# Moving small work between engines and timing every step by a table, in a two-layer graph kernel on one core

## The chip, the core and the metric

The kernel runs on one core of a Trainium2 chip. The core has a matmul engine (PE, with its weight loads as PEld), a vector engine (DVE), a scalar engine for activation functions (ACT), a general engine (POOL) and a queue for transfers (SP). Each works through its own instructions in program order and waits on semaphores for the others. The metric is the device time of one execution in microseconds; lower is better. Times come from three runs of the kernel, and one further execution was profiled.

## The reference

The input x has 32 batches of 512 channels by 1024 nodes; adj is a 512 by 512 matrix. Two layers follow each other, both on a layer norm over the nodes with a relu, and both with a residual:

```python
# layer 0
h = jnp.maximum(_layernorm(x, axis=-1), 0.0)
q = jnp.einsum('c,bcn->bn', wq, h)
k = jnp.einsum('c,bcn->bn', wk, h)
scores = q[:, None, :] + k[:, :, None]
scores = jnp.where(scores > 0, scores, 0.01 * scores)
att = jax.nn.softmax(scores, axis=-1)
agg = jnp.einsum('bcn,bmn->bcm', h, att)
out = jnp.einsum('oc,bcm->bom', adj, agg) + bm[None, :, None]
x = x + jax.nn.relu(out)
# layer 1
h = jnp.maximum(_layernorm(x, axis=-1), 0.0)
W = adj * adj
x = x + jnp.einsum('bnf,nm->bmf', h, W) + bias
```

## The kernel before, in words

A score is a leaky relu of q[n] + k[m]. For one row m the nodes n split into those with q[n] above -k[m] and those below, and in each part the exponential is a product of a factor of n and a factor of m. So the kernel sorts the nodes by q and needs, for each row, a sum over the nodes above a rank and another over those below. No 1024 by 1024 matrix of scores is made.

One batch goes through these steps, each a small function:

- load (four blocks of 128 channels), stats, norm, slopes, relu: layer norm and relu of layer 0, in place.
- scores and columns: q and k by matmuls, copied to the tile qr (line 216), through memory to all partitions (qrow), and transposed to columns (qk).
- rank (eight times): the place of each node in the order, by comparisons of qrow with a column of qk. Line 260 settles ties; it reads two tensors in on-chip memory, a slice of qrow and the mask before. lower (eight times, ACT, line 267): how many q lie below -k, by sums of signs.
- factors, to_rows, from_rows: small arithmetic that turns ranks into rows of a table td in memory (index idx) and into the rows to be read later (idg).
- value (eight times, PE, line 314): adj times h, 128 nodes at a time; spread copies it out of PSUM to the tile v; scatter (POOL, line 327) writes its rows, with q in the last column, to td in sorted order.
- fetch (SP, line 344): the sorted rows come back in nine groups, held in three tiles vs. weights: the factors of the nodes, as exponentials of the last column, copied first to the tile q (lines 351, 352). later: with w the weights, e is the sum of w over all later groups, made of eight additions one after another (line 369); wc are the weights with a one for the carry.
- totals: the running denominators by matmuls with masks, copied to den. stationary (POOL, line 387, three times): masks times weights, the stationary operand sm of three scans.
- scan (nine times, PE, line 397): a running sum of one group from above and of one from below, 64 partitions each. sums (nine times): ACT copies the two carries into the next groups' rows (lines 407, 408), then the whole result to the tile t (line 410); DVE copies the denominator into its last column (line 411); SP writes t to td (lines 413, 414).
- gather (POOL, eight times, line 419): for each node its row of running sums. excess and divide: the coefficients cf, with one exponential on ACT (line 430). combine (eight times): one multiplication on ACT (line 444), then two multiply-adds on DVE (line 446).
- turn (PE, line 453): transposes back; DVE adds the result, cut at zero, to the x that reload has brought again (tile y).
- stats, norm, slopes, relu for layer 1 (tile h); lift (POOL, line 205): adds bias to y; propagate (eight times, PE, line 460): W times h; finish (DVE, line 468): adds it to y, and SP writes y out.

Five batches are in the pipeline at once. The order of all instructions is written by hand: every step of batch b is put on a list with a planned time b * T + t, the list is sorted, and the steps are issued in this order, each engine's share of it being that engine's program. The planned times order the work and do nothing else. T is 80.57. In the last batches the late steps are moved forward by LAST and LAST_GAIN.

Buffers that matter here: PSUM has 8 banks, which all PE results share; t has 2 buffers, x and y have 7 tiles each of one channel block, g (the gathered rows of one batch) has one.

## Time and profile before

| What | us |
|---|---|
| median of three runs | 2488.57 (2484.91 to 2489.2) |
| the profiled execution | 2487.21 |
| its span, first to last instruction | 2485.5 |
| PE busy, granted clock 0.979 | 2358.2 |
| DVE busy | 2162.8 |
| ACT busy | 1458.2 |
| POOL busy | 992.7 |

The profile of one execution gives, for each engine, when each instruction ran. A group is a set of instructions of one line: after the bar come its busy time, the mean ns of one, then the idle time of the engine just before them and what ended most of it. A matmul in full precision appears as two passes, so value and propagate of one step are 8 records each. The records of a scan lie over each other; a scan takes 1.01 us from start to start. In 40 equal slices of the span, the busy tenths of three engines and the granted clock are:

```profile
PE   5789999999999999999999999999999999999788
DVE  6578999999999999999999999999999898888754
ACT  3666556566656566556566656566656566656441
...
PEclk9889999999999999999999999999999999999988
```

The transfers move 642.92 MB, at 259 GB/s in the mean, and the 16 transfer engines are busy for eight to nine tenths of most slices.

### The profile page before, as it was taken

How to read it: one execution, taken by the hardware profiler on the slowest of the kernel's cores; microseconds unless marked ns; L12 is line 12 of the kernel's file. 1: busy time of each engine (PE TensorE's matmuls, PEld its weight loads, DVE VectorE, ACT ScalarE, POOL GpSimd, SP SyncE). 2: the span in 40 equal slices, each digit the busy share in tenths (PEclk: the TensorE clock that was granted, in tenths of full speed). 3: DMA queues.
4: the chain of work that ended last, by engine and by line, in shares of the span. 5: the costliest groups of instructions: out<-in, count | busy, mean ns of one | idle time of the engine just before them, and what ended most of it. 6: DMA issues, size and time to landing. Idle time of an engine off the chain costs nothing. (4 is left out here: it accounts for less than half of the span.)

```text
span 2485.5 us, 28977 instructions
## 1 busy us (share of the span) xinstructions
PE 2358.2 (95%) x7632; PEld 991.0 (40%) x7632; DVE 2162.8 (87%) x5649; ACT 1458.2 (59%) x2341; POOL 992.7 (40%) x1101
## 2 busy tenths in 40 slices
PE   5789999999999999999999999999999999999788
PEld 2233444443444443344443444444344443444333
DVE  6578999999999999999999999999999898888754
ACT  3666556566656566556566656566656566656441
POOL 1234433344434334434334433345443334543431
PEclk9889999999999999999999999999999999999988
DMA  4698889898889888889888889898888888888772
GB/s 148 170 290 271 270 270 269 262 277 285 267 277 285 238 273 276 264 267 284 258 269 269 273 266 286 241 279 274 272 270 279 255 269 265 262 279 268 224 258 85
DMA packets 206528, 642.92 MB, mean 259 GB/s; under 512 B 29030, under 2 KB 29158, under 8 KB 206364
## 3 DMA queue, kind: packets, MB, share of 16 engines
q1 hardware_dynamic: 146704, 370.65, 53.9%
q0 software_dynamic: 57344, 268.99, 28.7%
q10 hardware_dynamic: 2316, 1.43, 0.3%
q8 instruction: 62, 1.02, 0.2%
q14 instruction: 102, 0.84, 0.1%
HBM read 429.94 MB, written 211.02 MB: 258 GB/s over the span
## 5 line engine op out<-in xcount | busy, mean ns | idle before, releaser
L460 PE MATMUL pg<-h,wsq 128*128 128x512 f32 x2048 | 936.8, 606 | 18.9 <-ACT h L199 18.6
L314 PE MATMUL pv<-wmT,x 128*128 128x512 f32 x2048 | 927.2, 601 | 24.3 <-ACT x L199 24.3
L419 POOL DMA_INDIRECT g<-td,idg x256 | 245.6, 959 | 1055.9 <-DVE e L369 498.0
L460 PEld LDWEIGHTS pg<-h,wsq 128*128 128x128 f32 x2048 | 378.8, 192 | 553.7 <-issue 462.8
L314 PEld LDWEIGHTS pv<-wmT,x 128*128 128x128 f32 x2048 | 375.2, 191 | 494.0 <-issue 444.8
L397 PE MATMUL sc<-vs,sm 128*64 128x512 f32 x1152 | 344.3, 636 | 67.6 <-ACT vs L407 49.2
L327 POOL DMA_INDIRECT td<-v,idx x256 | 275.8, 1077 | 319.8 <-issue 225.0
L446 DVE SCALAR_TENSOR_TENSOR g<-g,cf 128x512 f32<-128x512 f32 x512 | 375.4, 746 | 16.6 <-ACT g L444 7.6
L260 DVE SCALAR_TENSOR_TENSOR junk<-qrow,qk,before 128x128 bf16<-128x128 f32 x256 | 337.6, 1319 | 9.1
L205 POOL TENSOR_TENSOR y<-y,bias_sb 128x1024 f32<-128x1024 f32 x128 | 300.4, 2359 | 33.8 <-issue 30.6
L321 ACT COPY v<-pv 128x512 f32<-128x512 f32 x256 | 148.1, 579 | 275.8 <-PE pv L314 200.5
L267 ACT ACTIVATE junk<-qrow,qk 128x1024 bf16<-128x1024 f32 x256 | 292.5, 1142 | 0.1
L199 ACT ACTIVATE x<-x,nmr,rstd 128x1024 f32<-128x1024 f32 x128 | 151.7, 1236 | 138.2 <-DVE nmr L192 138.2
L468 DVE SCALAR_TENSOR_TENSOR y<-pg,bm_sb,y 128x512 f32<-128x512 f32 x256 | 188.2, 744 | 25.7 <-PE pg L460 25.7
L410 ACT COPY t<-sc 128x512 f32<-128x512 f32 x288 | 168.5, 585 | 45.8 <-PE sc L397 13.8
L256 DVE TENSOR_SCALAR_CACHE_REDUCE junk<-qrow,qk,cnt 128x896 bf16<-128x896 f32 (+6 forms) x224 | 180.5, 806 | 8.2
L455 DVE SCALAR_TENSOR_TENSOR y<-tr,nbm,y 128x512 f32<-128x512 f32 x256 | 177.8, 726 | 7.9 <-PE tr L453 7.9
L397 PEld LDWEIGHTS sc<-vs,sm 128*64 128x64 f32 x1152 | 66.1, 137 | 290.2 <-issue 122.5
L407 ACT COPY vs<-sc 1x512 f32<-1x512 f32 x256 | 144.6, 565 | 62.9 <-PE sc L397 62.9
L444 ACT ACTIVATE g<-g,cf 128x512 f32<-128x512 f32 x256 | 173.2, 715 | 3.2 <-DVE cf L438 3.2
L251 DVE TENSOR_SCALAR_CACHE_REDUCE junk<-qrow,qk 128x128 bf16<-128x128 f32 (+6 forms) x224 | 166.9, 745 | 3.5
L181 DVE BATCH_NORM_STATS2 st<-x 128x6 f32<-128x512 f32 x256 | 162.2, 675 | 3.5 <-DMA x<-in_x_dram 3.4
(106 smaller groups left out, 1885.2 us busy)
## 6 DMA issues: line engine op xcount, KB each, us to landing
vs<-td SPq DMA_DIRECT2D x192, 384.8 KB
td<-t SPq DMA_DIRECT2D x576, 128.2 KB
x<-in_x_dram SPq DMA_DIRECT2D x128, 512.0 KB
y<-in_x_dram SPq DMA_DIRECT2D x128, 512.0 KB
out_dram<-y SPq DMA_DIRECT2D x128, 512.0 KB
qrow<-qd SPq DMA_DIRECT2D x32, 512.0 KB
td<-v,idx POOLq DMA_INDIRECT x256, 5.3
g<-td,idg POOLq DMA_INDIRECT x256, 8.7
```

The costliest lines, as they stand in the source:

```text
L205: nc.gpsimd.tensor_tensor(s.x[c], s.x[c], bias_sb, ALU.add)
L256: nc.vector.tensor_scalar(junk[:, j * P :], s.qrow[:, j * P :], qc, first, ALU.is_lt, ALU.add, accum_out=s.cnt[:, 1, j : j + 1],)
L260: nc.vector.scalar_tensor_tensor(junk[:, ts(j, P)], s.qrow[:, ts(j, P)], qc, before, ALU.is_equal, ALU.mult, accum_out=s.cnt[:, 2, j : j + 1],
L267: nc.scalar.activation(junk, s.qrow, AF.Sign, bias=s.qk[:, 1, j : j + 1], accum_out=s.sgn[:, j : j + 1])
L314: nc.tensor.matmul(pv, s.h[c][:, ts(j, P)], wmT[:, c, :], start=(c == 0), stop=(c == NC - 1))
L327: i = nc.gpsimd.indirect_dma_start(tds[s.b % 3][:, :], bass.IndirectOffsetOnAxis(ap=s.idx[j // 4][:, j % 4 : j % 4 + 1], axis=0), v[:, :], ...
L397: nc.tensor.matmul(p[ts(k, HP), :], s.sm[i][k], s.vs[h][:, 0:C], start=True, stop=True)
L419: nc.gpsimd.indirect_dma_start(s.g[:, j, :], None, tds[s.b % 3][0 : 3 * NB * HP, :].rearrange("(s k) w -> s (k w)", k=3), bass.IndirectOff ...
L446: nc.vector.scalar_tensor_tensor(r, s.g[:, j, k * W : k * W + C], s.cf[:, k, j : j + 1], r, ALU.mult, ALU.add)
L455: nc.vector.scalar_tensor_tensor(xh, pt, nbm[:, o : o + 1], xh, ALU.max, ALU.add)
L460: nc.tensor.matmul(pg, wsq[:, r, ts(c, P)], s.h[r][:, ts(i, HALF)], start=(r == 0), stop=(r == NC - 1),)
L468: nc.vector.scalar_tensor_tensor(xh, s.pg.pop((c, i)), bm_sb[:, c : c + 1], xh, ALU.add, ALU.add)
```

## The change

Six edits. The bias addition lift goes from POOL to DVE. The copy of raw scores to qr goes from DVE to ACT. weights takes its exponentials straight from the fetched rows, six on ACT with three columns each instead of six copies and two exponentials; the weights are now kept in the opposite order of groups, with a zero in front of each half. later makes its sums over groups with one scan instruction. The denominator's copy into t goes from DVE to ACT. combine is split into weigh (ACT) and two separate multiply-adds (DVE). And every single step has a planned time of its own in a table, with T = 79.96, shifts for the first five batches and new ones for the last three; one load of batch 1 uses a buffer of y.

```diff
+PLAN = {
...
+    "excess": (197.53,),
...
+    "fetch": (74.37,),
...
+    "gather": (166.9, 167.4, 174.29, 175.46, 169.28, 190.2, 170.94, 177.02),
...
+    "norm0": (-13.33,),
+    "norm1": (246.23,),
...
+    "scan": (90.8, 98.9, 110.43, 116.3, 124.4, 137.24, 146.6, 154.57, 156.26),
...
+    "stationary": (87.74, 100.59, 124.44),
...
+    "sums": (91.04, 103.93, 115.73, 121.32, 128.67, 145.61, 149.72, 155.13, 157.36),
...
+    "turn": (230.81, 230.13, 230.45, 232.2, 233.84, 234.71, 233.3, 233.76),
...
+}
+LAST = (0.94, 0.36, 0.02,)
+LAST_KNOTS = (60, 95, 130, 150, 215, 250, 275, 300, 345, 400)
+LAST_GAIN = (0, 1.2, 5.7, 20.4, 20.4, 46.5, 53, 74.2, 87.6, 87.6)
+FIRST_KNOTS = (-60, 60, 150, 250, 350)
+FIRST_SHIFT = (
+    (1.7, -1.4, -0.5, -1.8, -0.5),
...
+)
...
+    zero = const.tile([P, 2], F32, name="zero")
+    nc.vector.memset(zero, 0.0)
+    runs = const.tile([P, 2 * (NB + 1)], F32, name="runs")
+    nc.vector.memset(runs, 1.0)
+    nc.vector.memset(runs[:, NB + 1 : NB + 2], 0.0)
...
     def load(s, c):
-        t = xp.tile([P, N], F32, tag="x", name=f"x_{s.b}_{c}")
+        pool, tag = (yp, "y") if (s.b, c) == (1, NC - 1) else (xp, "x")
+        t = pool.tile([P, N], F32, tag=tag, name=f"x_{s.b}_{c}")
...
     def lift(s, c):
-        nc.gpsimd.tensor_tensor(s.x[c], s.x[c], bias_sb, ALU.add)
+        nc.vector.tensor_tensor(s.x[c], s.x[c], bias_sb, ALU.add)
...
-        nc.vector.tensor_copy(s.qr, pq)
+        nc.scalar.copy(s.qr, pq)
...
     def weights(s):
-        q = sp.tile([P, 2, NB], F32, tag="q", name=f"q_{s.b}")
+        s.wz = sp.tile([P, 2, NB + 1], F32, tag="w", name=f"w_{s.b}")
+        s.w = s.wz[:, :, 1:]
+        nc.scalar.copy(s.wz[:, :, 0], zero)
         for i, t in enumerate(s.vt):
-            nc.vector.tensor_copy(q[:, 0, ts(i, 3)], t[:, :, C])
-            nc.vector.tensor_copy(q[:, 1, ts(NB // 3 - 1 - i, 3)], t[:, ::-1, C])
-        s.w = sp.tile([P, 2, NB], F32, tag="w", name=f"w_{s.b}")
-        nc.scalar.activation(s.w[:, 0, :], q[:, 0, :], AF.Exp, bias=s.nq[:, 0:1])
-        nc.scalar.activation(
-            s.w[:, 1, :], q[:, 1, :], AF.Exp, bias=s.nq[:, 1:2], scale=SLOPE
-        )
+            nc.scalar.activation(
+                s.w[:, 0, ts(NB // 3 - 1 - i, 3)], t[:, ::-1, C], AF.Exp, bias=s.nq[:, 0:1]
+            )
+            nc.scalar.activation(
+                s.w[:, 1, ts(i, 3)], t[:, :, C], AF.Exp, bias=s.nq[:, 1:2], scale=SLOPE
+            )
...
-        s.e = e = sp.tile([P, 2, NB], F32, tag="e", name=f"e_{s.b}")
-        nc.vector.memset(e, 0.0)
-        for h in range(NB - 2, -1, -1):
-            nc.vector.tensor_tensor(
-                e[:, :, h : h + 1], e[:, :, h + 1 : h + 2], s.w[:, :, h + 1 : h + 2], ALU.add
-            )
+        s.e = sp.tile([P, 2, NB + 1], F32, tag="e", name=f"e_{s.b}")
+        nc.vector.tensor_tensor_scan(
+            s.e.rearrange("p k g -> p (k g)"), runs, s.wz.rearrange("p k g -> p (k g)"),
+            0.0, ALU.mult, ALU.add,
+        )
...
-        nc.vector.tensor_copy(t[:, C:W], s.den[:, ha : ha + 1])
+        nc.scalar.copy(t[:, C:W], s.den[:, i : i + 1])
...
-    def combine(s, j):
+    def weigh(s, j):
         r = s.g[:, j, 0:C]
         nc.scalar.mul(r, r, s.cf[:, 0, j : j + 1])
-        for k in (1, 2):
-            nc.vector.scalar_tensor_tensor(
-                r, s.g[:, j, k * W : k * W + C], s.cf[:, k, j : j + 1], r, ALU.mult, ALU.add
-            )
+
+    def combine(s, j, k):
+        r = s.g[:, j, 0:C]
+        nc.vector.scalar_tensor_tensor(
+            r, s.g[:, j, k * W : k * W + C], s.cf[:, k, j : j + 1], r, ALU.mult, ALU.add
+        )
...
-    T = 80.57
+    def plan(s, f, name, *lead, args=None):
+        for n, t in enumerate(PLAN[name]):
+            at(s, t, f, s, *lead, *(args[n] if args else (n,)))
...
+    T = 79.96
```

In the order that the new table gives for a batch in the middle, PE runs, from its scores on: scores, value 3, columns, value 0, value 2, totals and scan 0 of the batch before, value 1, value 6, scan 1, value 7, value 4, value 5, then propagates and scans 2 to 6 in turn, a last pair of propagates among the transposes, scan 7, the transposes of one tile, scan 8. POOL runs gather 0, gather 1, stationary 0, then more gathers, stationary 3, the last gather and the scatters. In the order before, PE has its scans at even distances of 7.63 planned us, and POOL runs gather 0, then stationary 0, then the other gathers with three lifts among them.

## Prediction

> **What bounds the kernel now.** I read the page first: the busy shares and the costliest groups, then three stretches (start, middle, end), then the order of time in one period of the middle, then the waits of the middle. The page:

> ```profile
> span 2485.5 us, 28977 instructions
> PE 2358.2 (95%) x7632; PEld 991.0 (40%) x7632; DVE 2162.8 (87%) x5649; ACT 1458.2 (59%) x2341; POOL 992.7 (40%) x1101
> ...
> L260 DVE SCALAR_TENSOR_TENSOR junk<-qrow,qk,before 128x128 bf16<-128x128 f32 x256 | 337.6, 1319 | 9.1
> L205 POOL TENSOR_TENSOR y<-y,bias_sb 128x1024 f32<-128x1024 f32 x128 | 300.4, 2359 | 33.8 <-issue 30.6
> ```

> PE is full and DVE nearly so. One DVE group stands out: L260 reads only 128 columns and yet has a mean of 1319 ns; the list of its line gives a median of 354 and a maximum of 5374. The stretches (busy us of PE, PEld, DVE, ACT, POOL, then clock, DMA share, GB/s):

> ```profile
> 0.00:265.00 265.00, 211.72 (x680) 88.24 (x684) 190.59 (x585) 149.86 (x238) 78.59 (x115) 0.91 0.74 220
> 265.00:2266.00 2001.00, 1965.80 (x6425) 824.90 (x6423) 1838.64 (x4751) 1223.03 (x1971) 836.80 (x918) 0.99 0.87 270
> 2266.00:2486.00 220.00, 180.69 (x532) 77.83 (x530) 133.58 (x316) 85.28 (x132) 77.34 (x68) 0.91 0.61 206
> ```

> The middle holds 27 periods (first score matmul of batch 4 at 264.9, of batch 31 at 2266.5), 74.1 us each, with PE 98% busy. The order of time in one of them shows what PE still loses:

> ```profile
> 1247.87 5.36 DVE L260 SCALAR_TENSOR_TENSOR junk<-qrow,qk,before 128x128 bf16<-128x128 f32 x1
> ...
> 1264.97 2.36 POOL L205 TENSOR_TENSOR y<-y,bias_sb 128x1024 f32<-128x1024 f32 x1
> ...
> 1265.96 1.98 DVE L260 SCALAR_TENSOR_TENSOR junk<-qrow,qk,before 128x128 bf16<-128x128 f32 x1
> ...
> 1267.87 0.46 DVE L428 TENSOR_TENSOR cf<-g,arg 128x8 f32<-128x8 f32 x1
> ...
> 1268.56 0.21 ACT L430 ACTIVATE cf<-cf 128x8 f32<-128x8 f32 x1 [3.46 <-DVE cf L429]
> ...
> 1269.81 0.56 ACT L407 COPY vs<-sc 1x512 f32<-1x512 f32 x1
> ...
> 1270.42 1.67 PE L397 MATMUL sc<-vs,sm 128*64 128x512 f32 x4 [1.65 <-ACT vs L407]
> ```

> Read it downwards. A lift on POOL holds L260 on DVE (the 5.36 us one lies beside two lifts that run from 1248.39 to 1253.07). DVE comes late to the step excess (L428), ACT stands 3.46 us in its exponential (L430), the carry copies (L407) behind it come late, and scan 4 on PE waits 1.65 us. The waits of 300 to 2200 us say that it is so in every batch:

> ```profile
> PE sc L397 <- ACT vs L407: 32.1, 25, 3.5
> ACT cf L430 <- DVE cf L429: 92.0, 26, 5.1
> ```

> [...]

> **The parts of the change, per batch.**

> Lift moved from POOL to DVE. POOL loses 4 x 2.36 = 9.4 us. L260 falls from 1319 to about 354 ns: 8 x 0.965 = 7.7 us off DVE. DVE gains 4 x 1.22 = 4.9 us. If the price is wrong, 2.4 us (POOL's own) is the upper end: DVE then is up 1.9 net instead of down 2.8.

> Block sums as one scan. It removes 8 adds of 221 ns (L369) and a memset of 73: 1.8 us of busy time, 2.6 us of a dependent chain in the order of time. The scan instruction is in no row: between 0.15 (a one-column copy, L411) and 1.8 us (no gain); I take 0.3, for 20 columns.

> Raw scores and exponentials on ACT. DVE loses six copies of L351/L352 (0.93) and nine of L411 (1.3), and the score copy L216 (0.38). ACT gains the score copy, nine one-column copies, a zero copy and four more exponentials. The nearest row for the small ones is 0.19 to 0.30 (the accumulator read of L267 to L354), but back to back they stand about 0.1 to 0.2 apart: 0.3 + 9 x 0.12 + 0.1 + 4 x 0.2 = 2.3 us. In the new table the two square roots (norm0 66.6, norm1 6.4, in the period) no longer lie together between exponentials: weights 4.8, norm1, factors 34.9, norm0. That is four table loads instead of two, 2.6 us.

> Sums. DVE: 67.6 (2162.8/32) - 7.7 + 4.9 - 1.8 + 0.3 - 2.6 = 60.7 us. ACT: 45.6 + 4.9 = 50.5. POOL: 31.0 - 9.4 = 21.6. PE's instructions are the same, so PE is the bound, and only its stalls and order count.

> The table of all steps. I sorted both tables by time. PE's stream, without waits: 64 passes of value and of propagate at 0.43 us each, 9 scans of 1.01, 32 transposes of 0.109, scores 1.86, columns and totals 0.6, about 0.19 for each value or propagate that follows a scan or scores (9 before, 8 now): 71.6 us before, 71.4 now. So 2.5 us of 74.1 are loss today: 1.7 at scan 4 (shown above), 0.4 of clock (20 us at half clock in the middle, over 27), 0.4 of the rest.

> What is late next? I laid the new order out by hand, with the spacings of the order of time, PE from the start of scores at 0. DVE, 7 us lighter, has excess done at 37.5 and ACT asks for it at 39.2, so the stall at scan 4 should go. PE wants scan 0 at 13.0, scan 2 at 36, scan 5 at 49.6, scan 6 at 54.2, scan 7 at 68.8. ACT from scan 0 on is nearly unbroken (with relus at 1.14, sign sums at 1.14, sums at 1.8, spread at 0.48, weigh at 0.63): it reaches sums 4 at 47.2 and sums 5 at 52.6, so scan 6 has its carries at 53.8, 0.4 before PE wants them. Scan 8 has only the last transpose group (0.44) between itself and scan 7. In the trace a scan of 1.08, 0.07 to ACT, 0.61 to the first matmul of the next and 1.67 for that one give 3.4 us against 2.6 unhindered: a new stall of 0.85 us in each batch. With 0.4 of clock and 0.5 for the rest: 71.4 + 0.85 + 0.9 = 73.2 us, 0.9 less than now; 27 x 0.9 = 24 us.

> Start and end. The last batch's own chain loses 2.3 us in later, about 1 in weights (the copies) and some 2 of the lifts beside its ranks: 5 us. The new start shifts (FIRST_SHIFT) and the load of batch 1 into the y pool I cost at nothing, between -10 and +10: the first stretch has 53 us without PE, 28 of them before its first matmul and 24 lost to half clock, which no order removes. SP's queue: the load of block 3 of the next batch now stands in front of the rows of sums 2 and waits for value 5, the last reader of its buffer, at 32.5; sums 2 comes at 37, so it costs nothing. The fetch moves from 33 planned us ahead of scan 0 to 16; by my layout it is issued from 58 to 62, the one at 1289 to 1293 in the trace takes some 13 us to land, and weights wants it at 75, with 6 us more before scan 0 would wait: nothing, up to 1 us per batch if it lands at 82. PSUM: at most 7 of 8 banks are held at once in the new order (3 before), so no wait is forced there.

> Together 24 + 5 = 29 us: 2487.2 (the profiled execution; span 2485.5) - 29 = 2458. The median of the runs is 1.4 us higher: 2460.

> **Rivals.**

> Slower: POOL's queue. In the new order gather 0 and gather 1 of the older batch stand in front of stationary 0, whose product scan 0 needs. Gather 0 waits until the rows of sums 8 have landed: 7.7 us in the median from their last issue to gather 0, over the 32 batches (in the period above SP at 1227.24, POOL at 1234.60), the longest 9.9. By my layout the issue is 1.35 us after the end of scan 8, so gather 0 starts at 9.0, two gathers take 2.2, stationary 1.0: 12.3, and PE is there at 13.0. The slack is 0.7 us. From a landing of 8.4 us on, all of PE stands. At 10 us it costs 1.6 us per batch more: 74.8 instead of 73.2, 27 x 0.7 = 19 over now, less 5: 2502. For it: DMA is 0.87 busy, and the new order sends 1 MB of y tiles and the fetch shortly before. Against: 27 of the 32 are under 8.4.

> The same: ACT's chain. If sums 5 is 1.3 us later than laid out, scan 6 waits 0.9 us and the gain of the middle is gone: 2488 - 5 = 2484. Two things can do it: the nine small copies at 0.2 instead of 0.12 (0.5 by then), and t, which has two buffers: the copies of sums 4 need the landing of sums 2, which by the 7.7 us comes at 48, about when ACT asks. Against: the carries are copied before t.

> Much faster: the stall at scan 8 is covered, because ACT works ahead and PE never catches up elsewhere, and the residue halves: 72.1 us, 27 x 2 = 54, and 5 to 10 at the ends: 2427. For it: every engine but PE has over 12 us of room.

> **How the numbers follow.** Forecast 0.47 (2440 to 2478), much faster 0.20, ACT's chain 0.10 (2474 to 2492), POOL's queue 0.23. A measurement of this kernel tells 0.2% (5 us) from no change. The ACT rival is split 0.03 faster, 0.05 same, 0.02 slower; of POOL's queue 0.01 ends in same. Faster 0.70, same 0.06, slower 0.24. The predicted time is 2460; the range goes from the much faster case, 2425, to the worst landing, 2502.

> **What would show it.** In the new profile: the L260 group near 360 ns; lift on DVE at 1.2 to 1.3 us; DVE near 60.7 us x 32 = 1940 busy; ACT near 1620; table loads near 128 (67 and two singles before); the wait of the scan matmuls for L407 moved to one scan per batch, the last; PE busy share up by about 1%. The forecast is wrong if scan matmuls wait for POOL (then it is the queue), if DVE stays above 2050, or if the period is above 74.

## The result and the profile after

| | Before | After |
|---|---|---|
| median of the runs, us | 2488.49 (4 runs) | 2415.81 (4 runs) |
| span of the profiled execution, us | 2485.5 | 2415.1 |
| PE, DVE, ACT, POOL busy, us | 2358, 2163, 1458, 993 | 2344, 1932, 1591, 705 |
| granted clock, mean | 0.979 | 0.984 |

The ratio is 0.9708 (95% interval 0.9691 to 0.9724): 73 us less, where 28 were forecast, and below the range. The page of the changed kernel, the lines that answer to those of before:

```profile
span 2415.1 us, 28224 instructions
PE 2343.5 (97%) x7632; PEld 986.1 (41%) x7632; DVE 1932.3 (80%) x5012; ACT 1591.2 (66%) x2879; POOL 704.7 (29%) x973
...
L263 DVE TENSOR_TENSOR y<-y,bias_sb 128x1024 f32<-128x1024 f32 x128 | 153.4, 1220 | 4.5 <-ACT h L257 4.5
```

Its groups, with shapes kept apart (count, then busy us and mean ns):

```profile
L318 DVE SCALAR_TENSOR_TENSOR junk<-qrow,qk,before 128x128 bf16<-128x128 f32 x256 | 94.4, 369 | 9.1
L426 DVE TENSOR_TENSOR_SCAN e<-runs,w 128x20 f32<-128x20 f32 x32 | 6.1, 191 | 0.0
```

The tie step (L260 before, L318 now) takes 369 ns instead of 1319, the lift 1220 ns on DVE, the scan instruction 191 ns. The three stretches, cut at the first score matmul of batch 4 and of batch 31 (columns as before):

```profile
0.00:259.00 259.00, 210.43 (x668) 85.67 (x668) 172.84 (x512) 156.10 (x284) 70.94 (x111) 0.89 0.74 225
259.00:2209.00 1950.00, 1948.09 (x6430) 820.78 (x6429) 1619.74 (x4211) 1343.14 (x2431) 592.16 (x810) 1.00 0.88 277
2209.00:2416.00 207.00, 184.95 (x540) 79.67 (x538) 139.69 (x292) 91.96 (x165) 41.61 (x52) 0.95 0.63 217
```

The middle of 27 periods fell from 2001.6 to 1949.7 us, 51.9 less; PE is busy for 1948 of 1950 us, at a granted clock of 1.00. From batch 8 on the periods are 72.3 us each, but for the last, 71.6. In the old order one value (3.5 us) precedes the scores of its batch and in the new one none; with that set right, the start gained 264.9 - 3.5 - 259.3 = 2.1 us and the end 219.0 + 3.5 - 206.1 = 16.4. The sum is the 70.4 by which the span fell.

The waits of 300 to 2200 us (total, times, longest):

```profile
POOL sm L445 <- PE sc L455: 135.8, 26, 5.8
...
ACT cf L488 <- DVE cf L487: 4.4, 2, 2.2
```

ACT's wait for excess, 92 us before, is 4.4. POOL waits for scans of PE to give up a buffer of sm; no scan waits for POOL. What PE still loses shows in the order of time at the end of a period:

```profile
1266.14 1.08 PE L455 MATMUL sc<-vs,sm 128*64 128x512 f32 x4
1267.15 0.66 PE L513 MATMUL tr<-ident,g 128*128 128x128 f32 x4
1267.27 0.58 ACT L465 COPY vs<-sc 1x512 f32<-1x512 f32 x1 [8.14 <-PE sc L455]
...
1267.87 0.58 ACT L466 COPY vs<-sc 1x512 f32<-1x512 f32 x1
...
1267.90 1.67 PE L455 MATMUL sc<-vs,sm 128*64 128x512 f32 x4
...
1268.50 0.19 PEld L455 LDWEIGHTS sc<-vs,sm 128*64 128x64 f32 x2 [0.41 <-ACT vs L466]
```

Scan 7, one group of transposes, then scan 8, which starts when the first carry is copied and takes 1.67 us instead of 1.08 because its second half waits for the second one (L466). PE stands idle for less than 0.1 us before it, so nearly all of this stall of 0.7 us lies in the length of the scan and counts as busy. The prediction laid it out at 0.85.

### The profile page after: what moved, and what is told of

Read it like the earlier page. It is cut to its first block, busy times and chain, and to the rows that moved or that the text cites. A ratio compares the mean times of both kernels' runs of the same rounds, so it can differ in the third digit from the quotient of the medians.

```text
span 2415.1 us, 28224 instructions
## 1 busy us (share of the span) xinstructions
PE 2343.5 (97%) x7632; PEld 986.1 (41%) x7632; DVE 1932.3 (80%) x5012; ACT 1591.2 (66%) x2879; POOL 704.7 (29%) x973
## 4 chain that ended last, share of the span: by engine, by line
PE 92%; ACT 2%; DMA 2%; DVE 1%; issue 1%; POOL 0%; SPq 0%; ACTq 0%; POOLq 0%; DVEq 0%
PE pv L372 37%; PE pg L520 35%; PE sc L455 13%; PE tr L513 4%; PE pq L269 2%; DMA vs<-td 1%; ACT vs L465 1%; DMA g<-td,idg 1%; ACT x L257 1%; ACT g L502 0%; DVE y L515 0%; DMA td<-pad 0%; PE pd L434 0%; PE pr L283 0%; DMA bm_sb<-in_L_gnn_bm_dram 0%
## 5 line engine op out<-in xcount | busy, mean ns | idle before, releaser
L372 PE MATMUL pv<-wmT,x 128*128 128x512 f32 x2048 | 912.0, 599 | 0.0
L385 POOL DMA_INDIRECT td<-v,idx x256 | 286.7, 1120 | 571.2 <-ACT g L502 186.5
L465 ACT COPY vs<-sc 1x512 f32<-1x512 f32 x256 | 145.7, 569 | 418.1 <-PE sc L455 417.8
L506 DVE SCALAR_TENSOR_TENSOR g<-g,cf 128x512 f32<-128x512 f32 x512 | 350.0, 747 | 24.8 <-ACT g L502 24.5
L314 DVE TENSOR_SCALAR_CACHE_REDUCE junk<-qrow,qk,cnt 128x640 bf16<-128x640 f32 (+6 forms) x224 | 180.5, 806 | 8.2
L309 DVE TENSOR_SCALAR_CACHE_REDUCE junk<-qrow,qk 128x384 bf16<-128x384 f32 (+6 forms) x224 | 165.9, 740 | 9.3 <-DMA qrow<-qd 7.9
L502 ACT ACTIVATE g<-g,cf 128x512 f32<-128x512 f32 x256 | 163.9, 715 | 2.6 <-DVE cf L496 2.6
L239 DVE BATCH_NORM_STATS2 st<-y 128x6 f32<-128x512 f32 x256 | 160.6, 669 | 0.0
L263 DVE TENSOR_TENSOR y<-y,bias_sb 128x1024 f32<-128x1024 f32 x128 | 153.4, 1220 | 4.5 <-ACT h L257 4.5
L466 ACT COPY vs<-sc 1x512 f32<-1x512 f32 x256 | 147.7, 577 | 5.5
L257 ACT ACTIVATE h<-y,nmr,rstd 128x1024 f32<-128x1024 f32 x128 | 149.2, 1237 | 2.9 <-PE pg L520 2.3
```

Of the source, the lines that this page charges most:

```text
L239: nc.vector.bn_stats(st[:, i, :], s.x[c][:, ts(i, HALF)])
L257: nc.scalar.activation(h, s.x[c], AF.Relu, bias=s.nmr[:, c : c + 1], scale=s.rstd[:, c : c + 1])
L314: nc.vector.tensor_scalar(junk[:, j * P :], s.qrow[:, j * P :], qc, first, ALU.is_lt, ALU.add, accum_out=s.cnt[:, 1, j : j + 1],)
L372: nc.tensor.matmul(pv, s.h[c][:, ts(j, P)], wmT[:, c, :], start=(c == 0), stop=(c == NC - 1))
L385: i = nc.gpsimd.indirect_dma_start(tds[s.b % 3][:, :], bass.IndirectOffsetOnAxis(ap=s.idx[j // 4][:, j % 4 : j % 4 + 1], axis=0), v[:, :], ...
L506: nc.vector.scalar_tensor_tensor(r, s.g[:, j, k * W : k * W + C], s.cf[:, k, j : j + 1], r, ALU.mult, ALU.add)
```

## The experiments

Two theories stood at the start. By the first (placement), the lifts on POOL, which hold the tie step on DVE, are the cause of the loss before, and taking them off POOL is the gain. By the second (order), the table is the gain. The prediction and two of the expectations call the scan that waits in the kernel before scan 4; counted from 0 as everywhere else it is scan 5. The matmuls of totals, which stand behind scan 0 in the old order, follow the first scan of the period (1239.31 us), and the one that waits at 1270.42 is the sixth.

Each ratio is to the kernel before as it ran beside the changed one, with medians of 2482.9 to 2487.9 us. A few us between two rows lie inside the intervals; where they matter, the periods of the traces decide.

| Kernel | Median, us | Ratio to before (95%) | Middle period, us |
|---|---|---|---|
| e1 lift only, old order | 2421.0 | 0.9741 (0.9704 to 0.9779) | 71.8 |
| e2 changed, lift back on POOL | 2419.7 | 0.9736 (0.9698 to 0.9774) | 72.3 |
| e3 table only | 2438.0 | 0.9812 (0.9774 to 0.9851) | 72.3 |
| e4 all placements, old order | 2419.0 | 0.9731 (0.9693 to 0.9770) | 71.8 |
| e5 changed, scan 7 earlier | 2400.2 | 0.9662 (0.9644 to 0.9681) | 71.6 |
| e6 other placements, old order | 2480.0 | 0.9981 (0.9966 to 0.9996) | 73 to 76 |
| e9 changed, no end shifts | 2444.3 | 0.9834 (0.9793 to 0.9875) | 72.3 |
| e10 changed, no start shifts | 2420.3 | 0.9741 (0.9700 to 0.9782) | 72.3 |
| e11 changed, additions back | 2416.7 | 0.9728 (0.9688 to 0.9769) | 72.3 |
| e12 as e4, no end shifts | 2432.5 | 0.9778 (0.9758 to 0.9797) | 71.8 |

**e1: lift alone.**

```diff
-        nc.gpsimd.tensor_tensor(s.x[c], s.x[c], bias_sb, ALU.add)
+        nc.vector.tensor_tensor(s.x[c], s.x[c], bias_sb, ALU.add)
```

> The kernel before with only lift moved to DVE, the old order kept. Placement theory (lifts on POOL held the tie step L260 on DVE, and through excess and the carries scan 4): L260 falls to about 0.36 us in the mean, the stall of 1.7 us at scan 4 goes, the middle period falls from 74.1 to about 72.5 us, 2440 to 2455 us in all. Order theory (the table brings the gain, the placement only makes room): period within 0.4 us of 74.1, 2478 to 2490.

Measured 2421.0, a larger gain than the placement theory asked for: 62 us against the 2482.9 of the kernel before that ran beside it. Its groups, and ACT's wait for excess from 300 to 2200 us (92.0 us in all before):

```profile
L205 DVE TENSOR_TENSOR y<-y,bias_sb 128x1024 f32<-128x1024 f32 x128 | 157.2, 1231 | 2.1 <-ACT h L199 2.1
L260 DVE SCALAR_TENSOR_TENSOR junk<-qrow,qk,before 128x128 bf16<-128x128 f32 x256 | 91.0, 355 | 9.2
```

```profile
ACT cf L430 <- DVE cf L429: 56.5, 27, 2.8
```

And the stretch of 300 to 2200 us:

```profile
300.00:2200.00 1900.00, 1900.00 (x6299) 802.68 (x6298) 1682.62 (x4754) 1206.78 (x1931) 579.76 (x790) 1.00 0.90 278
```

PE does not pause once in 1900 us, and every period is 71.8 us. So in the old order one moved instruction takes away all that PE lost in the middle: 2001.6 against 1937.6 us over the 27 periods, 2.4 us a batch, and not only the 1.7 at which the prediction had put the stall.

Moving lift also empties POOL's queue, in which three lifts stood among the gathers that excess needs. That isn't what made excess late: in every period of the middle before, the last gather had landed at least 8.3 us when excess started. DVE comes to it earlier now: in the mean of the middle excess starts 41.5 us after the latest score matmuls in the kernel before, and 36.0 us in e1.

**e2: lift put back into the changed kernel.** The diff of e1, reversed.

> The changed kernel with only lift put back on POOL, the new order kept. Placement theory: the tie step or another two-input step on DVE is held again, and 25 us or more of the 73 are lost (over 2440). Order theory: in the new order the lifts stand beside other work and little is lost, under 2426.

Measured 2419.7; the 4 us to the changed kernel are inside the intervals. The tie step is held again, but excess is not late, and the period is 72.3 as in the changed kernel:

```profile
L318 DVE SCALAR_TENSOR_TENSOR junk<-qrow,qk,before 128x128 bf16<-128x128 f32 x256 | 162.0, 633 | 9.2
```

```profile
ACT cf L488 <- DVE cf L487: 5.2, 3, 2.7
```

Here the order theory is right.

**e3: the table alone.** All placements of before in the changed kernel, as the diff of the change reversed for lift, scores, weights, later, stationary and sums.

> The new table, with all placements of before (lift on POOL, raw scores, exponential inputs and denominators on DVE, additions instead of the scan instruction). Placement theory: 2450 to 2490, since the holds are still there. Order theory: 2415 to 2432.

Measured 2438.0, between the ranges of the two theories. Its group of the tie step, and its wait for excess from 300 to 2200 us:

```profile
L313 DVE SCALAR_TENSOR_TENSOR junk<-qrow,qk,before 128x128 bf16<-128x128 f32 x256 | 199.9, 781 | 9.1
```

```profile
ACT cf L483 <- DVE cf L482: 7.5, 3, 3.1
```

The holds are there, yet ACT hardly waits, and from batch 8 on the period is 72.3. The first periods are longer (76.9, 72.0, 73.7, 73.8) and the end is 217.6 us instead of 206.1. So order and placement each cure the stall, and their gains (45 and 62 us against the kernel before that ran beside them) don't add.

**e4: all placements, old order.** e1 and the other placements together; the old combine and the old table.

> All new placements with the old order, and old LAST. Placement theory: the middle gains nearly all of its 52 us and the ends some 5, 2430 to 2442. Order theory: no better than 2475.

Measured 2419.0, better than expected: the old order with all moves can't be told from the changed kernel by its time. Its middle is the shorter one, by 0.5 us a batch; the new table loses that at scan 8 and wins it back at the ends.

**e5: one number of the table.**

```diff
-    "scan": (90.8, 98.9, 110.43, 116.3, 124.4, 137.24, 146.6, 154.57, 156.26),
+    "scan": (90.8, 98.9, 110.43, 116.3, 124.4, 137.24, 146.6, 154.2, 156.26),
```

> The changed kernel with one number of the table changed: scan 7 goes ahead of the last propagate, so that 3.5 us of matmuls lie between it and scan 8. If the 0.9 us that PE loses at scan 8 in each batch is that carry, the middle period falls from 72.3 to 71.4 to 71.6 us and the whole by 17 to 25, to 2391 to 2399. If another wait follows at once, the period stays above 72.

Measured 2400.2, a microsecond above the expected range, with periods of 71.6. Its order of time at the end of a period:

```profile
1183.26 1.08 PE L455 MATMUL sc<-vs,sm 128*64 128x512 f32 x4
1184.27 3.70 PE L520 MATMUL pg<-h,wsq 128*128 128x512 f32 x8
1187.81 0.60 PE L513 MATMUL tr<-ident,g 128*128 128x128 f32 x4
1188.34 1.08 PE L455 MATMUL sc<-vs,sm 128*64 128x512 f32 x4
```

The propagate lies over the two carries, and scan 8 takes 1.08 us again. The 0.7 us by which the period falls are what the stall cost. It is the fastest kernel of this study, 16 us below the changed one.

**e6: the other placements without lift, old order.** e4 with lift left on POOL.

> The kernel before, old order, lift left on POOL, with the other placements only (raw scores, exponentials and denominators on ACT, the scan instruction). They take 4.4 us of work off DVE in each batch but leave the holds of L260. If DVE's lateness is a sum, whatever it is made of, the stall at scan 4 (1.7) shrinks or goes: 2425 to 2445. If the holds themselves decide, because they lie just before excess: over 2465.

Measured 2480.0, under 0.2% from before. DVE is busy for 2069.1 us instead of 2162.8, 2.9 us less in each batch (4.4 is the sum of its instructions, which lie over each other in part: in the trace before all of DVE's sum to 2422.7 us and keep it busy for 2162.8). In e1, for comparison, it is busy 3.6 us less. The waits of 300 to 2200 us are what they were:

```profile
ACT cf L435 <- DVE cf L434: 96.4, 26, 5.2
PE sc L402 <- ACT vs L412: 37.1, 25, 3.0
```

The tie step's mean even rose, from 1319 to 1340 ns. That fits a hold that lasts until POOL's lift is over: a lighter DVE only comes to it sooner. Excess starts 41.6 us after the scores in the mean, as before (41.5). So DVE was not late because of how much it had to do.

**e7 and e8: the price of a pause of PE.** In the changed kernel, further copies of t in front of the carries of sums 7, 2 in e7 and 5 in e8:

```diff
+        t = tp.tile([P, W], F32, tag="t", name=f"t_{s.b}_{i}")
+        for _ in range(5 if i == NB - 2 else 0):
+            nc.scalar.copy(t[:, 0:C], p)
         if i < NB - 1:
...
-        t = tp.tile([P, W], F32, tag="t", name=f"t_{s.b}_{i}")
```

> The changed kernel with two more copies of t in front of the carries of sums 7, in each batch, so that PE pauses about 1.1 us before scan 8. If a pause costs only itself: period 72.3 + 0.97 = 73.3 us. If pauses of 2 us and more also bring a stretch at half clock (as five of the six longest of the middle did before, 1.94 to 3.53 us, and none of the nine between 1.08 and 1.79), this one is too short for it: the same 73.3, clock 1.00 in the middle.

> The same with five more copies: PE pauses about 2.5 us before scan 8. If a pause costs only itself: 72.3 + 2.4 = 74.7 us and clock 1.00 in the middle. If such a pause brings 3.4 us of half clock: another 1.7, 76.4 us, and a clock of about 0.98 in the middle.

Each copy delayed the carries by 0.6 us, not 0.48, so the pauses were 1.22 and 3.08 us. Each of the two kernels ran once. e7 took 2452.4 us with periods of 73.5 and a granted clock of 1.00 from 300 to 2200 us: the pause cost itself. e8 took 2531.8 us. Its periods are 75.3 where the clock stayed (72.3 and the 3.0 of the copies) and up to 78.0 where it did not. One pause, in the order of time, and the clock (the last but two columns) before and after it:

```profile
1321.00 0.65 PE L515 MATMUL tr<-ident,g 128*128 128x128 f32 x4
1324.73 2.02 PE L455 MATMUL sc<-vs,sm 128*64 128x512 f32 x4 [3.08 <-ACT vs L468]
```

```profile
1310.00:1324.70 14.70, 11.66 (x53) 6.45 (x51) 10.99 (x28) 6.37 (x9) 0.00 (x0) 1.00 0.93 229
1325.90:1329.30 3.40, 3.40 (x30) 1.25 (x32) 2.75 (x6) 0.76 (x3) 0.00 (x0) 0.50 0.53 122
```

Between 600 and 2200 us 11 of 21 such pauses came with 3.4 or 6.8 us at half clock, 47.8 us together, and the 21 periods are 76.25 us in the mean, 0.9 more than the 75.3. Which pauses these are is told in the last section.

**e9 and e12: the end shifts.** LAST made empty in the changed kernel (e9) and in e4 (e12).

> The changed kernel without the shifts of the last batches (LAST empty). If the 16 us that the end gained come from them: 2430 or more, with the middle unchanged at 72.3 us. If the gain at the end comes from the table itself and the lighter DVE: within 5 us of 2416.

> All new placements with the old order, and without the old LAST. It tells what the old end shifts were worth, beside 28 us of the new ones (2444.3 without, 2415.8 with). If the old table needs about as long an end as the new one when neither is shifted: 2435 (16 us above 2419), and the 12 us by which the new end is shorter belong to the new shifts. If the old shifts were worth as much as the new: 2445 or more, and the new end is shorter by its table.

The new shifts are worth 28.5 us (2444.3 - 2415.8), the old ones 13.5 (2432.5 - 2419.0). Without shifts the two ends are alike, 233.7 us (e9) and 227.8 + 3.5 = 231.3 (e12). So in these executions the table itself gives the end nothing; the new shifts do, by 15 us more than the old.

**e10: the start shifts.** FIRST_SHIFT made empty, and the load of batch 1 into the x pool.

> The changed kernel without the start shifts and with the load of batch 1 back in the x pool. The prediction put them at nothing, between -10 and +10: 2406 to 2426. The first 190 us tell it; the middle stays at 72.3 us.

Measured 2420.3, 4.5 us more, inside the expected range. The first stretch, to which the expectation pointed, is no longer (259.4 us to the scores of batch 4, 259.3 in the changed kernel). The middle is longer by 2.3 us, since the changed kernel runs its first four periods of it at 71.5 to 71.9 and this one has 72.3 throughout. Why a shift of the start keeps the stall at scan 8 away for four batches was not tried.

**e11: the additions back.**

```diff
-        nc.vector.tensor_tensor_scan(
-            s.e.rearrange("p k g -> p (k g)"), runs, s.wz.rearrange("p k g -> p (k g)"),
-            0.0, ALU.mult, ALU.add,
-        )
+        nc.vector.memset(e, 0.0)
+        for h in range(1, NB):
+            nc.vector.tensor_tensor(
+                e[:, :, h : h + 1], e[:, :, h - 1 : h], s.wz[:, :, h : h + 1], ALU.add
+            )
```

> The changed kernel with the eight additions in place of the scan instruction. If it is worth only its place in the last batch's own chain: middle 72.3 us as before, the end 1.5 to 2.5 us later, 2417 to 2419. If it makes room that the middle needs: 2425 or more.

Measured 2416.7 (2414.8 to 2419.7), which can't be told from 2415.8 (2411.7 to 2416.8). The scan instruction saves 1.3 us of DVE's busy time in each batch (1973.7 against 1932.3 in all) and moves the time by nothing that was measured.

## Why the prediction was wrong

**Right: the mechanism of the middle.** The chain from the lifts over the tie step, excess and the carries to scan 5 is what PE lost time to, and e1 takes it away by its first link alone. PE is the bound after; the scans wait for neither POOL nor ACT's long chain. The hand-laid order was good: scans 2, 5, 6 and 7 were put at 36, 49.6, 54.2 and 68.8 us after the scores and start at 35.8, 49.8, 54.5 and 68.6. The new stall at scan 8 was laid out at 0.85 us and is 0.7; e5 shows that it is the carry.

**Right: the parts.** The 1.22 us for lift on DVE, my estimate (the nearest instruction of the trace before, L237 on DVE with 1024 columns in, took 1209 ns), was 1.220, the tie step "near 360" is 369, DVE "near 1940" is 1932, ACT "near 1620" is 1591. The scan instruction was taken at 0.3 and is 0.19. Table loads, forecast at 128, are 127, each of 1283 ns as in the trace before, where 35 stand at the square root (L186), 32 at the exponential of the weights (L354), and the two singles at other exponentials.

**Wrong by size: the residue.** The step that failed is "With 0.4 of clock and 0.5 for the rest: 71.4 + 0.85 + 0.9 = 73.2". The measured period is 72.3. I carried both terms over from before as if they were a property of the chip and of the run, and neither was there:

- The clock term is nothing. In e1 and the changed kernel, where PE pauses for no more than 0.1 us in the middle, the granted clock there is 1.00 (300 to 2200 us and 259 to 2209 us).
- The rest was in part a slip in the sum. The terms of PE's stream as the prediction lists them (128 passes, 9 scans, 32 transposes, scores, columns and totals, and 0.19 nine or eight times) add up to 71.8 before and 71.6 now, not to 71.6 and 71.4. 71.8 is the period of e1, and 71.6, the period of e5, is also what the changed kernel has without its stall: 71.6 + 0.7 = 72.3. (Such a sum is good to 0.1 or 0.2 us.)
- What remained of the rest belonged to the stall. The prediction took 1.7 us for it from the idle time of one period. Over the 27 periods before, PE is idle for 1.3 us in the mean, its scans 4 and 5 are 0.7 us longer than 1.08 because they wait for the second carry, and half of the 20 us at half clock is 0.4 us a period. That is 2.4, all that e1 regains.

At 27 periods the 0.9 us are 24 of the 41 us that the sum missed (70.4 - 29); some 4 more come from the periods at 71.5 to 71.9 and from rounding.

**Wrong by size: the ends.** They were put at 5 us and gave 18.5: 2.1 at the start and 16.4 at the end. The end's sum counted only durations in the last batch's own chain. e1 and e4 show that this part is about right: with all placements and the old order the end falls from 222.5 to 217.9, 4.6 us. The other 12 come from the new end shifts, on which the prediction put no price at all: by e9 and e12 they are worth 15 us more than the old, on an unshifted end that is 2.4 us longer. The order of the last batches was never laid out as that of the middle was.

At the start the prediction counts 24 us as "lost to half clock, which no order removes". That reading is off: the first stretch has 58 us at half clock in the changed kernel and 27 in e9, whose start is the same, and it lasts 259.3 and 258.7 us. In these runs half clock at the start doesn't set its length.

**The rivals.** POOL's queue in front of stationary 0 is not there: no scan waits for POOL in the middle, and stationary 0 is done 2.8 us or more before scan 0, where 0.7 was laid out. ACT's chain is not there either: scan 6 is at most 0.2 us longer than 1.08. "Much faster" came nearest in its number (2427), but not by its reason: the stall at scan 8 was not covered. (Its own terms, 71.4 and half of the residue, give 71.9 and not 72.1.) The prediction's sum gave the middle's gain to the placement alone. The runs say that the table by itself also ends the stall (e3), and that on top of the placement it costs the middle 0.5 us a batch (e4 against the changed kernel). Which of its many numbers takes excess out of the ranks' way no run splits.

## What to carry to other kernels

A stall in a full engine can be more than the idle time before one instruction: here 1.3 us of idle time came with 0.7 by which the scans themselves were longer and 0.4 of half clock, in the mean of all periods. In e1 all 2.4 us of it went, and the period fell to the 71.8 us of the stream's sum, so add that sum up with care. Ask of a late engine whether it works or is held: here 2.9 us less to do in each batch changed next to nothing, and another engine's 9.4 us of work, which took the late one 4.9, took away 62 us when moved onto it. In an order written by hand, put something long between a result and the next step that needs it, and lay out the last batches by themselves, since the shifts of the end alone were worth 28 us.

## What the hardware showed that was not expected

In the kernel before, a pause of PE could cost nearly twice its length. One of 2.06 us is followed by a stretch at half clock, in which another 1.7 us, half of its 3.4, are lost (order of time, then the clock as the last column but two):

```profile
1345.02 2.41 PE L397 MATMUL sc<-vs,sm 128*64 128x512 f32 x4 [2.06 <-ACT vs L407]
```

```profile
1345.80:1349.20 3.40, 3.40 (x5) 0.85 (x4) 3.33 (x8) 3.40 (x7) 2.83 (x5) 0.50 0.83 224
```

In the kernel before, half clock followed a window that was idle for all of its 3.41 us, and also two that were idle for 2.04 and 2.06.

The hold of the tie step by a lift lasted until the lift was over, not for a share of it. The tie step of 5.36 us that the prediction shows (the median of its line is 0.354) began at 1247.87 and ended 0.16 us after these two lifts:

```profile
1248.39 4.68 POOL L205 TENSOR_TENSOR y<-y,bias_sb 128x1024 f32<-128x1024 f32 x2
```

Of the 256 tie steps before, 45 began while a lift ran, and none of them ended before that lift did. L256 on DVE, which reads a slice of qrow and no second tensor of its size, was not held: of its 32 instructions with 128 columns 26 began inside a lift and took 405 ns in the mean, and so did the 6 others.
